# First transfers, token copies and bias stores of an attention and expert kernel, put in another order

## The chip, the cores and the metric

The kernel runs on one core of a Trainium2 chip. The core has a matrix engine (TensorE, "PE" in the profile, with its weight loads as "PEld"), a vector engine (VectorE, "DVE"), ScalarE ("ACT"), GpSimd ("POOL") and SyncE ("SP"), which here only issues DMA. ScalarE and GpSimd issue DMA as well. Each engine runs its own queue of instructions in order; semaphores tie the queues together. The metric is the device time of one execution in microseconds, and the median over the executions is what counts.

## The reference

The computation has two parts: an attention over 16 sequences of 512 tokens (width 512, 16 heads of 64, one shared key and value head, a null key, an additive bias and a causal mask), and a layer of 16 experts in which each expert picks its own 512 tokens. The tokens `x` themselves are added to the result.

```python
xn = layernorm(x, g_in)
q = (xn @ Wq).reshape(b, n, H, DH).transpose(0, 2, 1, 3) * scale
kv = xn @ Wkv                              # k, v: one head, with a null key and value put in front
sim = einsum('bhid,bjd->bhij', q, k) + bias
sim = where(causal_mask, neg, sim)         # causal, the same for all sequences
sim = where(mask_p[:, None, None, :], sim, neg)
out = einsum('bhij,bjd->bhid', softmax(sim), v) @ Wo
a = layernorm(out, g_out)
...
logits = rmsnorm(a) @ router_weight.T + router_bias
_, idx = top_k(logits.T, 512)              # each of 16 experts takes 512 of the 8192 tokens
y = gelu(xe @ fc1.T + b1) @ fc2.T + b2     # per expert
output = scatter_add(y * gates) / gate_sums
return x + output
```

The bias (16 heads, 512 x 512) is the same for every sequence; so is the causal mask, and so is their combination.

## The kernel before, in words

**Attention: 16 sequences of 8 head pairs.** A loop over `p` = 0 to 128 handles pair `p` (sequence `p // 8`, two heads) and, in the same turn, parts of its neighbours. For pair `p` TensorE makes the scores in PSUM (`sp`), VectorE adds the bias and takes the row minimum in one instruction (`reduce`, four query blocks in the order 3, 2, 0, then 1), ScalarE takes the exponentials and normalizes. In the next turn (`behind`) VectorE transposes the probabilities in squares of 32 x 32 (`turn`: six instructions into the buffer `sq`, of which there is only one), and 16 DMAs of 80 KB move the squares to their places (`move`, `sq` to `pt`): ten are issued by SP and six by POOL. In the turn after that (`turned`) TensorE multiplies them with the values (`attend`, `ap`). Beside this the turn makes the queries of the next pair (`qp`), normalizes and transposes the token tiles of the next sequences (`InNorm`, with its inverse root `ln_r` on POOL), and projects and routes the previous sequence.

**Order.** The helper class `Pinned` (line 119) keeps what TensorE, VectorE, ScalarE and GpSimd are given in the order of the program text. SP is not pinned: `nc.sync` is ordered by the scheduler of the framework. A tile that has a fixed number of buffers makes its next writer wait for the last reader: two for a token tile `x`, two for a bias tile.

**Bias.** `load_bias(p)` (line 227) is called in turn `p - 1`. For the first eight pairs it loads 1280 KB (1.3 MB) of bias, has POOL fill the upper triangle of the four diagonal blocks with a large negative number (`affine_select`), and stores the result to the memory tensor `causal`; from pair 8 on the masked bias is loaded from there. In POOL's order these four masks of pair `p + 1` stand ahead of the six moves of turn `p`; the store is issued by SP.

**Tokens.** `Sequence.load` (line 251) loads a tile of 128 tokens (256 KB) into SBUF and copies it from there to the output, so that the experts can later add to it. The first sequence's four tiles are loaded ahead of the loop, the next one's also before the loop, the others two turns ahead of their normalization.

**Constants.** ScalarE issues all the weight loads at the start (lines 163 to 184): input gain, key and value weights, null key and value, 2 MB of query weights, the null bias, 2 MB of output weights `wo`, the gains and the router. VectorE then negates `vk_col` and the null bias (`nn_sb`), makes the first sequence's mask (`km`), and only then starts the first normalizations (lines 610 to 618). The transposed tokens (`turn`, line 259) pass through one PSUM buffer.

**Experts.** After attention and the choice of tokens come 16 experts, in which the two layers' products follow one another on TensorE; nothing in that part is touched.

Of the kernel before, what the change touches and what calls it, by code (L numbers as in the profile page):

```python
# [8 lines left out]
F32 = mybir.dt.float32  # L9
# [4 lines left out]
AF = mybir.ActivationFunctionType  # L14
ALU = mybir.AluOpType
# [4 lines left out]
P = 128  # L20
EPS = 1e-5

BIG = float(2.0**100)
# [3 lines left out]
def tile_adaln_ffn(  # L27
# [36 lines left out]
    scale = DH ** -0.5  # L64
# [21 lines left out]
    causal = dram.tile([HP, P, 2, SW], F32, name="causal")  # L86
# [22 lines left out]
        base=-1, channel_multiplier=-1,  # L109
# [9 lines left out]
    class Pinned:  # L119
# [4 lines left out]

        def __getattr__(self, name):
            made = getattr(self.engine, name)
            return lambda *args, **kwargs: tc.keep_in_program_order(made(*args, **kwargs))  # L127

    te, ve, se, ge = [Pinned(a) for a in (nc.tensor, nc.vector, nc.scalar, nc.gpsimd)]


    with ExitStack() as st:
# [27 lines left out]
        rw_sb = const.tile([P, DC, E], F32, name="rw_sb")  # L160
        rb_sb = const.tile([P, E], F32, name="rb_sb")

        nc.scalar.dma_start(out=g_in_sb, in_=g_in)
        for j in range(2):
            nc.scalar.dma_start(
                out=wvk_sb[:, :, j * DH : (j + 1) * DH], in_=wkv_c[:, :, (1 - j) * DH : (2 - j) * DH]
            )
            nc.scalar.dma_start(
                out=vk_col[j * DH : (j + 1) * DH, :],
                in_=null_kv[1 - j].rearrange("(d o) -> d o", o=1),  # L170
            )
        for c in range(DC):
            nc.scalar.dma_start(out=wq_sb[:, c, :], in_=wq[c * P : (c + 1) * P, :])
        nc.scalar.dma_start(out=nb_sb, in_=null_bias.partition_broadcast(P))

        for j in range(2):
            nc.scalar.dma_start(
                out=nv_col[j * DH : (j + 1) * DH, :], in_=null_kv[1].rearrange("(d o) -> d o", o=1)
            )
        nc.scalar.dma_start(out=wo_sb, in_=wo.rearrange("(c p) n -> p c n", p=P))  # L180
        nc.scalar.dma_start(out=g_out_sb, in_=g_out.partition_broadcast(P))
        nc.scalar.dma_start(out=nw_sb, in_=norm_w.partition_broadcast(P))
        nc.scalar.dma_start(out=rw_sb, in_=router_w.rearrange("(c p) e -> p c e", p=P))
        nc.scalar.dma_start(out=rb_sb, in_=router_b.partition_broadcast(P))

        mhalf = const.tile([P, 1], F32, name="mhalf")
        nc.vector.memset(mhalf, -0.5)
# [38 lines left out]

        def load_bias(p):


            bt = biasp.tile([P, 2, SW], F32, name=f"bias_{p}", tag="bias")  # L230
            if p >= HP:
                nc.sync.dma_start(out=bt, in_=causal[p % HP])
                return bt
            nc.sync.dma_start(out=bt, in_=bias[p])
            for q in range(QB):
                diag = bt[:, :, off[q] + ext[q] - P : off[q] + ext[q]]
                ge.affine_select(
                    out=diag, in_=diag, pattern=[[0, 2], [-1, P]],
                    compare_op=ALU.is_ge, fill=-BIG, base=0, channel_multiplier=1,
                )  # L240
            nc.sync.dma_start(out=causal[p], in_=bt)
            return bt

        class Sequence:

# [5 lines left out]
            def load(self, t):  # L251
                b = self.b
                rows = slice(b * N + t * P, b * N + (t + 1) * P)
                xt = work.tile([P, D], F32, name=f"x_{b}_{t}", tag="x")
                nc.sync.dma_start(out=xt, in_=x_t[rows, :])
                nc.sync.dma_start(out=out_t[rows, :], in_=xt)
                self.xts[t] = xt

            def turn(self, t):
                if t == 0:  # L260
                    self.xnt = seq.tile([P, DC, N], F32, name=f"xnt_{self.b}", tag="xnt")
                tp = ps_t.tile([P, DC, P], F32, name=f"xtp_{self.b}_{t}", tag="t")
                for c in range(DC):
                    te.transpose(tp[:, c, :], self.xns[t][:, c * P : (c + 1) * P], ident)
                ve.tensor_tensor(
                    self.xnt[:, :, t * P : (t + 1) * P], tp,
                    g_in_sb.unsqueeze(2).to_broadcast([P, DC, P]), ALU.mult,
                )

            def mask(self):  # L270
                m8 = small.tile([DH + 1, N], U8, name=f"m8_{self.b}", tag="m8", bufs=1)
# [335 lines left out]
        for t in range(QB):  # L607
            seqs[0].load(t)
        biases = {0: load_bias(0)}
        ve.tensor_scalar_mul(vk_col, vk_col, -1.0)  # L610
        ve.tensor_scalar_mul(nn_sb, nb_sb, -1.0)
        seqs[0].mask()
# [17 lines left out]
        for p in range(B * HP + 1):  # L630
            b, hp = divmod(p, HP)
            now, ahead = ahead, None
            if p + 1 < B * HP:
                biases[p + 1] = load_bias(p + 1)
                ahead = Pair(seqs[(p + 1) // HP], (p + 1) % HP)
            for c, t in loads.get(p, ()):
                seqs[c].load(t)
            bt = biases.pop(p, None)
            chains = [InNorm(seqs[c], t) for c, t in ins.get(p, ())]
            if p in norms:  # L640
                chains.append(OutNorm(seqs[norms[p][0]], norms[p][1]))
            second = steps(*[seqs[c].project(*divmod(h, 2)) for c, h in halves.get(p, ())])
            asked = ahead.queries() if ahead else steps()

            if now:
                now.scores(3)
                now.scores(2, 0)
                now.reduce(3, bt)
                now.exps(3)
# [53 lines left out]
        ve, se, ge = nc.vector, nc.scalar, nc.gpsimd  # L703
        for t in range(QB):
            last.project_part(t, range(early, HP))
            n = OutNorm(last, t)
# [609 lines left out]
```

## Time and profile before

| | |
|---|---|
| median of 3 runs | 3651.52 us (3649.92 to 3652.57) |
| profiled execution | 3655.35 us, its span 3653.6 us |
| mean granted TensorE clock | 0.977 |
| PE busy | 3441.1 us (94%) |
| DVE busy | 2330.9 us (64%) |
| ACT busy | 1585.2 us (43%) |
| POOL busy | 894.3 us (24%) |
| first score matmul of pair 0 | 49.5 us |
| first score matmul of pair 8 | 171.1 us |
| end of attention | about 1940 us |
| SP's DMA queue | 473.44 MB, 39.0% of 16 engines' span |
| POOL's DMA queue | 101.29 MB, 12.3% |
| ACT's DMA queue | 5.53 MB, 0.4% |

Busy times overlap, since the engines work beside each other. What an engine's idle time costs depends on who waits for it, so the profile is read by stages: TensorE has gaps in the first 200 us and between about 1940 and 2130 us, and is full elsewhere. Queues named SPq, ACTq and POOLq show the issue of a DMA, not its movement of data.

### The profile page before, as it was taken

The page shows a single profiled execution, that of the slowest core. Times are in us where ns is not written, and L with a number is a line of the kernel's source. Part 1 is how long each engine was busy: PE and PEld are TensorE (multiplying, and loading weights), DVE is VectorE, ACT ScalarE, POOL GpSimd, SP SyncE. Part 2 cuts the span into 40 slices and gives each one's busy share as a digit, 9 for nine tenths or more (in the row PEclk, how much of TensorE's full clock was granted, in tenths as well). Part 3 has the DMA queues.
Part 4 walks back from the last instruction along what each step waited for, and adds up shares of the span by engine and source line. Part 5 has one row for each costly group of instructions (what it writes and reads, how often), then busy time and mean ns, then how long its engine had stood idle before and what let it go on. Part 6 is the DMA issues. An engine that isn't in the chain of part 4 may idle for free.

```text
span 3653.6 us, 52226 instructions
## 1 busy us (share of the span) xinstructions
PE 3441.1 (94%) x16972; PEld 2478.7 (68%) x16972; DVE 2330.9 (64%) x6028; ACT 1585.2 (43%) x4152; POOL 894.3 (24%) x1314
## 2 busy tenths in 40 slices
PE   5799999999999999999993699999999999999998
PEld 2355556555565555555552488888888888888887
DVE  4567676777667767767656865555565666555553
ACT  3567676676666766667660111111121111111111
POOL 2232332332332323233320222111121122222110
PEclk9799999999999999999996799999999999999999
DMA  7777666676667676676642233333333334333330
GB/s 251 241 212 225 207 205 209 211 221 214 203 208 222 213 212 205 205 214 198 196 148 104 70 118 110 104 93 94 115 122 119 119 122 122 110 122 110 112 91 12
DMA packets 263286, 583.58 MB, mean 160 GB/s; under 512 B 49255, under 2 KB 118023, under 8 KB 245607
## 3 DMA queue, kind: packets, MB, share of 16 engines
q1 hardware_dynamic: 215680, 473.44, 39.0%
q0 software_dynamic: 42960, 101.29, 12.3%
q10 hardware_dynamic: 4375, 5.53, 0.4%
q8 instruction: 136, 2.23, 0.3%
q14 instruction: 135, 1.11, 0.1%
HBM read 349.64 MB, written 61.87 MB: 113 GB/s over the span
## 4 chain that ended last, share of the span: by engine, by line
PE 50%; DVE 5%; issue 1%; DMA 1%; POOL 0%; ACT 0%; SPq 0%; DVEq 0%; POOLq 0%; ACTq 0%
PE r_y L127 9%; PE pc L127 6%; PE pc_y L127 6%; PE pa_y L127 6%; PE pa L127 6%; PE pe L127 3%; PE pb L127 3%; PE pd L127 3%; PE op L127 2%; PE qp L127 2%; PE sp L127 1%; PE ap L127 1%; DVE sel L836 1%; PE xgp L127 1%; DVE sq L127 1%
## 5 line engine op out<-in xcount | busy, mean ns | idle before, releaser
L127 ACT ACTIVATE p<-p,nm 128x512 f32<-128x512 f32 (+3 forms) x1024 | 561.9, 550 | 243.8 <-DVE nm L127 242.5
L127 DVE CUSTOM_DVE_ANT_0 p<-sp,bias,nn_sb 128x512 f32<-128x512 f32 (+3 forms) x1024 | 500.5, 546 | 174.1 <-PE sp L127 174.0
L127 POOL DMA_DIRECT2D pt<-sq x762 | 381.6, 508 | 877.6 <-issue 559.8
L127 PE MATMUL qp<-xnt,wq_sb 128*128 128x512 f32 x1024 | 512.2, 623 | 0.0
L127 PE MATMUL op<-wo_sb,ot 128*128 128x256 f32 x1920 | 457.0, 382 | 8.8 <-ACT ot L127 8.6
L127 PEld LDWEIGHTS op<-wo_sb,ot 128*128 128x128 f32 x1920 | 357.4, 190 | 109.3 <-issue 54.3
L127 DVE STREAM_TRANSPOSE sq<-p 128x896 f32<-128x896 f32 x762 | 398.7, 589 | 49.8 <-DMA pt<-sq 27.5
L127 ACT ACTIVATE p<-p,rs 128x512 f32<-128x512 f32 (+2 forms) x768 | 406.2, 603 | 1.9 <-DVE rs L127 1.1
L127 POOL DMA_INDIRECT out_dram<-y,tok x64 | 106.2, 1659 | 1184.3 <-ACT y L1145 1184.3
L1053 ACT ACTIVATE h<-h,b_sb 128x512 f32<-128x512 f32 (+1 forms) x256 | 143.4, 607 | 529.1 <-DVE h L127 471.1
L127 PE MATMUL sp<-ka,qa 64*128 64x512 f32 (+3 forms) x2048 | 357.7, 440 | 1.8 <-ACT qa L127 1.8
L127 PE MATMUL ap<-pt,vp 128*64 128x512 f32 (+3 forms) x2048 | 310.8, 446 | 18.6 <-DMA pt<-sq 9.1
L1145 ACT ACTIVATE y<-y,gg 128x512 f32<-128x512 f32 x64 | 46.2, 722 | 647.3 <-DVE y L127 647.3
L127 PEld LDWEIGHTS qp<-xnt,wq_sb 128*128 128x128 f32 x1024 | 174.9, 190 | 183.2 <-issue 167.8
L127 PEld LDWEIGHTS ap<-pt,vp 128*64 128x64 f32 x2048 | 148.8, 139 | 195.4 <-issue 158.1
L127 PE MATMUL pa<-xe,w 128*128 128x256 f32 x1024 | 243.5, 381 | 0.0
L127 PEld LDWEIGHTS sp<-ka,qa 64*128 64x128 f32 x2048 | 174.2, 190 | 87.5 <-issue 81.5
L127 PE MATMUL pa_y<-w,h 128*128 128x256 f32 x1024 | 231.5, 379 | 0.0
L127 PE MATMUL r_y<-w2t,hs 128*128 128x256 f32 x1024 | 231.5, 379 | 0.0
L127 PEld LDWEIGHTS pa<-xe,w 128*128 128x128 f32 x1024 | 195.9, 191 | 27.0
L127 PEld LDWEIGHTS r_y<-w2t,hs 128*128 128x128 f32 x1024 | 194.6, 190 | 26.5
L127 PEld LDWEIGHTS pa_y<-w,h 128*128 128x128 f32 x1024 | 193.4, 190 | 25.7
(191 smaller groups left out, 5191.6 us busy)
## 6 DMA issues: line engine op xcount, KB each, us to landing
bias<-causal SPq DMA_DIRECT2D x120, 1280.0 KB
w<-in_fc_dram SPq DMA_DIRECT2D x256, 512.0 KB
pt<-sq SPq DMA_DIRECT2D x1270, 80.0 KB
pt<-sq POOLq DMA_DIRECT2D x762, 80.0 KB
x<-in_x_dram SPq DMA_DIRECT2D x64, 256.0 KB
out_dram<-x SPq DMA_DIRECT2D x64, 256.0 KB
table<-xf SPq DMA_DIRECT2D x64, 256.0 KB
bias<-in_bias_dram SPq DMA_DIRECT2D x8, 1280.0 KB
```

The source lines that it names most:

```text
L127: return lambda *args, **kwargs: tc.keep_in_program_order(made(*args, **kwargs))
L836: nc.vector.tensor_scalar(flags, l2, than, None, op, ALU.add, accum_out=red)
L1053: nc.scalar.activation(a[0], a[1], AF.Gelu, bias=b1_sb[:, self.e, f : f + 1])
L1145: nc.scalar.activation(y, y, AF.Copy, scale=self.gg[:, g, self.e : self.e + 1])
```

## The change

- The four token tiles of the first sequence become SP's first transfers, into four buffers of their own (`x` and `xf`). ScalarE now issues only the key and value weights, the input gain and the query weights, these in two parts by columns (the first two pairs' first). The small vectors are issued by POOL. `wo`, the gains and the router weights go to `later_weights`, issued by POOL in turn 1.
- The first normalizations stand ahead of `nn_sb`, `km` and `vk_col` on VectorE. The first sequence's odd tiles go through another PSUM pool and are scaled by ScalarE in four pieces.
- SP is pinned too (`sy`), so its transfers keep the order of the text.
- `load_bias` only loads. `mask_bias(p + 1)` stands behind the moves of turn `p`; POOL masks and then issues the store to `causal`.
- Token tiles are no longer copied to the output from SBUF. In turns 8 to 71 SP copies one tile of 128 rows from the input tensor to the output tensor, memory to memory, behind its moves. Token loads stand behind the moves too, and the second half of the second sequence is loaded in turn 0 instead of before the loop.

TensorE's instructions keep their order.

```diff
+            def call(*args, **kwargs):
+                self.last = tc.keep_in_program_order(made(*args, **kwargs))
+                return self.last
...
+    te, ve, se, ge, sy = [
+        Pinned(a) for a in (nc.tensor, nc.vector, nc.scalar, nc.gpsimd, nc.sync)
+    ]
...
-        nc.scalar.dma_start(out=g_in_sb, in_=g_in)
+        x0 = {}
+        for t in range(QB):
+            x0[t] = work.tile([P, D], F32, name=f"x_0_{t}", tag="x" if t < 2 else "xf")
+            nc.sync.dma_start(out=x0[t], in_=x_t[t * P : (t + 1) * P, :])
...
-        for c in range(DC):
-            nc.scalar.dma_start(out=wq_sb[:, c, :], in_=wq[c * P : (c + 1) * P, :])
-        nc.scalar.dma_start(out=nb_sb, in_=null_bias.partition_broadcast(P))
+        for cols in (slice(0, 2 * P), slice(2 * P, H * DH)):
+            nc.scalar.dma_start(out=wq_sb[:, :, cols], in_=wq_c[:, :, cols])
...
+        nc.gpsimd.dma_start(out=nb_sb, in_=null_bias.partition_broadcast(P))
...
+        def later_weights():
+            ge.dma_start(out=wo_sb, in_=wo.rearrange("(c p) n -> p c n", p=P))
+            ge.dma_start(out=g_out_sb, in_=g_out.partition_broadcast(P))
+            ge.dma_start(out=nw_sb, in_=norm_w.partition_broadcast(P))
+            ge.dma_start(out=rw_sb, in_=router_w.rearrange("(c p) e -> p c e", p=P))
+            ge.dma_start(out=rb_sb, in_=router_b.partition_broadcast(P))
...
-            nc.sync.dma_start(out=causal[p], in_=bt)
+            sy.dma_start(out=bt, in_=causal[p % HP] if p >= HP else bias[p])
             return bt
+        def mask_bias(p, bt):
+            with tc.issue_after(ge.last.ins):
+                for q in range(QB):
+                    diag = bt[:, :, off[q] + ext[q] - P : off[q] + ext[q]]
+                    ge.affine_select(
...
+            ge.dma_start(out=causal[p], in_=bt)
...
-                nc.sync.dma_start(out=xt, in_=x_t[rows, :])
-                nc.sync.dma_start(out=out_t[rows, :], in_=xt)
+                sy.dma_start(out=xt, in_=x_t[rows, :])
...
+                if odd:
+                    for c in range(DC):
+                        se.activation(dst[:, c, :], tp[:, c, :], AF.Copy, scale=g_in_sb[:, c : c + 1])
...
-            loads.setdefault(max(p - 2, -1), []).extend(tiles)
+            loads.setdefault(max(p - 2, min(p - 1, 0)), []).extend(tiles)
...
         for pair in ((0, 1), (2, 3)):
...
+        mask_bias(0, biases[0])
+        ve.tensor_scalar_mul(vk_col, vk_col, -1.0)
         for t in range(QB):
             seqs[0].turn(t)
+        ve.tensor_scalar_mul(nn_sb, nb_sb, -1.0)
+        seqs[0].mask()
...
-                behind.move(nc.sync, range(6, SN * SN))
+                behind.move(sy, range(6, SN * SN))
                 behind.move(ge, range(6))
+            if p + 1 < HP:
+                mask_bias(p + 1, biases[p + 1])
+            if p == 1:
+                later_weights()
+            if 0 <= p - HP < NT // P:
+                rows = slice((p - HP) * P, (p - HP + 1) * P)
+                sy.dma_start(out=out_t[rows, :], in_=x_t[rows, :])
+            for c, t in loads.get(p, ()):
+                seqs[c].load(t)
```

More of the change, by code (lines that the diff above doesn't have):

```diff
@@ L126, in __getattr__ @@
             made = getattr(self.engine, name)
-            return lambda *args, **kwargs: tc.keep_in_program_order(made(*args, **kwargs))
-    te, ve, se, ge = [Pinned(a) for a in (nc.tensor, nc.vector, nc.scalar, nc.gpsimd)]
+            def call(*args, **kwargs):
+                self.last = tc.keep_in_program_order(made(*args, **kwargs))
+                return self.last
+            return call
+    te, ve, se, ge, sy = [
+        Pinned(a) for a in (nc.tensor, nc.vector, nc.scalar, nc.gpsimd, nc.sync)
+    ]
     with ExitStack() as st:
@@ L167, in tile_adaln_ffn @@
             )
-            nc.scalar.dma_start(
+        nc.scalar.dma_start(out=g_in_sb, in_=g_in)
+        wq_c = wq.rearrange("(c p) n -> p c n", p=P)
+        for cols in (slice(0, 2 * P), slice(2 * P, H * DH)):
+            nc.scalar.dma_start(out=wq_sb[:, :, cols], in_=wq_c[:, :, cols])
+        for j in range(2):
+            nc.gpsimd.dma_start(
                 out=vk_col[j * DH : (j + 1) * DH, :],
@@ L171, in tile_adaln_ffn @@
             )
-        for c in range(DC):
-            nc.scalar.dma_start(out=wq_sb[:, c, :], in_=wq[c * P : (c + 1) * P, :])
-        nc.scalar.dma_start(out=nb_sb, in_=null_bias.partition_broadcast(P))
+        nc.gpsimd.dma_start(out=nb_sb, in_=null_bias.partition_broadcast(P))
         for j in range(2):
-            nc.scalar.dma_start(
+            nc.gpsimd.dma_start(
                 out=nv_col[j * DH : (j + 1) * DH, :], in_=null_kv[1].rearrange("(d o) -> d o", o=1)
             )
[L180 to L184, printed above, removed]
+        def later_weights():
[4 more added lines that the diff above has]
+            ge.dma_start(out=rb_sb, in_=router_b.partition_broadcast(P))
         mhalf = const.tile([P, 1], F32, name="mhalf")
@@ L230, in load_bias @@
             bt = biasp.tile([P, 2, SW], F32, name=f"bias_{p}", tag="bias")
[L231 to L241, printed above, removed]
-            return bt
+            sy.dma_start(out=bt, in_=causal[p % HP] if p >= HP else bias[p])
+            return bt
+        def mask_bias(p, bt):
[3 more added lines that the diff above has]
+                    ge.affine_select(
+                        out=diag, in_=diag, pattern=[[0, 2], [-1, P]],
+                        compare_op=ALU.is_ge, fill=-BIG, base=0, channel_multiplier=1,
+                    )
+            ge.dma_start(out=causal[p], in_=bt)
         class Sequence:
@@ L261, in turn @@
                     self.xnt = seq.tile([P, DC, N], F32, name=f"xnt_{self.b}", tag="xnt")
-                tp = ps_t.tile([P, DC, P], F32, name=f"xtp_{self.b}_{t}", tag="t")
+                odd = self.b == 0 and t % 2 == 1
+                pool, tag = (ps_m, "m") if odd else (ps_t, "t")
+                tp = pool.tile([P, DC, P], F32, name=f"xtp_{self.b}_{t}", tag=tag)
                 for c in range(DC):
                     te.transpose(tp[:, c, :], self.xns[t][:, c * P : (c + 1) * P], ident)
[L265 to L268, printed above, removed]
+                dst = self.xnt[:, :, t * P : (t + 1) * P]
+                if odd:
+                    for c in range(DC):
+                        se.activation(dst[:, c, :], tp[:, c, :], AF.Copy, scale=g_in_sb[:, c : c + 1])
+                else:
+                    ve.tensor_tensor(
+                        dst, tp, g_in_sb.unsqueeze(2).to_broadcast([P, DC, P]), ALU.mult
+                    )
             def mask(self):
@@ L604, in tile_adaln_ffn @@
         for p, tiles in ins.items():
-            loads.setdefault(max(p - 2, -1), []).extend(tiles)
-        for t in range(QB):
-            seqs[0].load(t)
+            loads.setdefault(max(p - 2, min(p - 1, 0)), []).extend(tiles)
+        seqs[0].xts = x0
         biases = {0: load_bias(0)}
-        ve.tensor_scalar_mul(vk_col, vk_col, -1.0)
-        ve.tensor_scalar_mul(nn_sb, nb_sb, -1.0)
-        seqs[0].mask()
         for pair in ((0, 1), (2, 3)):
@@ L635, in tile_adaln_ffn @@
                 ahead = Pair(seqs[(p + 1) // HP], (p + 1) % HP)
-            for c, t in loads.get(p, ()):
-                seqs[c].load(t)
             bt = biases.pop(p, None)
@@ L702, in tile_adaln_ffn @@
         last = seqs[end]
-        ve, se, ge = nc.vector, nc.scalar, nc.gpsimd
+        ve, se, ge, sy = nc.vector, nc.scalar, nc.gpsimd, nc.sync
         for t in range(QB):
```

## The prediction

> **What bounds the kernel now.** I read the windows of busy time first, to find where TensorE is not full; then, in those places, the instructions in order of time, engine by engine.
>
> ```profile
> 50.00:100.00 50.00, 37.61 (x167) 16.64 (x168) 34.54 (x116) 30.80 (x93) 11.62 (x25) 0.88 0.70 228
> 100.00:150.00 50.00, 35.44 (x152) 16.97 (x151) 26.06 (x84) 26.95 (x72) 14.24 (x32) 0.84 0.73 232
> 150.00:200.00 50.00, 41.67 (x192) 20.62 (x194) 32.23 (x106) 29.81 (x84) 14.67 (x31) 0.87 0.77 240
> ...
> 500.00:1000.00 500.00, 491.73 (x2590) 291.04 (x2590) 353.07 (x1164) 350.33 (x975) 158.69 (x280) 1.00 0.69 212
> ```
>
> The columns are stretch, its length, busy time of PE, weight loads, DVE, ACT and POOL, granted clock, DMA share, GB/s. From 200 us to the end of attention (about 1940 us) PE is 98% busy: nothing in its instruction order changes, so there I count zero. Up to 200 us it is not full and its clock falls below 1.0. A loss there is never made up, so a gain there comes out at the end one for one. Two things leave it empty. The first is the start:
>
> ```profile
> 19.48 0.17 DVE L127 TENSOR_SCALAR nn_sb<-nb_sb 128x16 f32<-128x16 f32 x1 [8.29 <-DMA nb_sb<-in_null_bias_dram]
> 20.42 0.69 DVE L127 BATCH_NORM_STATS2 ln_s<-x 128x6 f32<-128x512 f32 x1
> 23.23 1.76 SPq L255 DMA_DIRECT2D x<-in_x_dram  x2
> 29.41 0.69 DVE L127 BATCH_NORM_STATS2 ln_s<-x 128x6 f32<-128x512 f32 x1 [4.77 <-DMA x<-in_x_dram]
> 38.60 5.93 PE L127 MATMUL kp<-xnt,wvk_sb 128*128 128x256 f32 x16
> ```
>
> Each row: start, duration, instruction, and in brackets the idle time before it with what ended it. The first normalization (20.42) stands in DVE's queue behind the negated null bias, whose transfer lies behind 2 MB of wq. Token tiles 2 and 3 are asked for only at 23.23, when two buffers come free. The second is pairs 2 to 7:
>
> ```profile
> 76.47 3.14 DVE L127 STREAM_TRANSPOSE sq<-p 128x896 f32<-128x896 f32 x6 [0.76 <-DMA pt<-sq]
> 79.64 0.51 SPq L517 DMA_DIRECT2D pt<-sq  x1
> 82.33 0.34 SPq L256 DMA_DIRECT2D out_dram<-x  x1
> 82.99 0.39 SPq L241 DMA_DIRECT2D causal<-bias  x1
> 83.42 9.36 SPq L517 DMA_DIRECT2D pt<-sq  x9
> 92.90 0.52 SPq L234 DMA_DIRECT2D bias<-in_bias_dram  x1
> 95.24 3.14 DVE L127 STREAM_TRANSPOSE sq<-p 128x896 f32<-128x896 f32 x6 [9.20 <-DMA pt<-sq]
> 95.27 4.54 PE L127 MATMUL ap<-pt,vp 128*64 128x512 f32 x16 [7.27 <-DMA pt<-sq]
> ```
>
> This is one turn of a loop: transposed squares, ten moves on SP (six on POOL beside them), landing, next transposes, since there is one squares buffer. After the first move SP waits for a token tile, then for the mask, issues the 1.3 MB store, and its other nine moves queue behind that store at 1.04 us each.
>
> **The loop in numbers.** Call T_k the start of pair k's transposes: T_0 to T_6 are 63.28, 76.47, 95.24, 112.44, 131.57, 150.84, 166.93. From T_1 to T_6 a pair takes 90.5/5 = 18.1 us. From the end of the transposes (T_k + 3.1) to the end of the last SP move: 13.2, 12.0, 13.9, 13.7 and 11.3 us for k = 1 to 5. But 8.4 for k = 0 (66.45 to 74.80: the store had gone ahead at 64.33 and nothing stood among the moves), and 7.0 in a later pair without stores:
>
> ```profile
> 625.45 3.13 DVE L127 STREAM_TRANSPOSE sq<-p 128x896 f32<-128x896 f32 x6
> ...
> 628.65 6.89 SPq L517 DMA_DIRECT2D pt<-sq  x10
> ```
>
> From the last move to the next transposes it takes 2.5, 2.1, 2.1, 2.4, 1.6, mean 2.1.
>
> **The change, part by part.**
>
> *Start.* The four token loads go first on SP, 0.43 each: all issued by 2.5 us. DMA moved 203 GB/s in 0 to 5 us and 304 in 5 to 10, so 1.0 and 2.5 MB by then; if ScalarE's queue (wvk, wq) takes half, the 1.05 MB of tokens are through when 2.1 MB are, at 8.6, and landed at about 10.5 (estimate; ends 8.6 and 12). The second pair of normalizations took 29.41 to 33.24 = 3.8, so xn_3 is ready at 14.4; the last turn is 1.11, and the key matmuls start at 15.5 instead of 38.60. The two turns given to ScalarE (eight pieces; the nearest row, its copy of 128x256, 0.37) end under the first half of those matmuls, 2.9 us. The five small loads that POOL now issues (0.5 each by its moves) end before the first ln_t, so they cost nothing; without that cover, 2.5. From there to the first score reduction, 12.8 us (38.60 to 51.41), nothing moves. **Gain 23** (ends 20 and 25).
>
> *Bias 1 and 2.* Bias 1 is now issued behind the ka moves, near 23; with two token tiles ahead it is 1.8 MB, at 383 GB/s (65 to 70 us) 4.8, landed about 30, masked by 32; pair 1 wants it at 60.32 - 23 = 37.3. Cost 0, cover 5. Bias 2 stands on SP behind two token loads that wait for the pair 0 normalization (60.0 - 23 = 37.0): issued 38.4, landed about 45. Its mask waits for POOL's moves of pair 0 (to 47) and ends at 48.5; pair 2 wants it at 49.7. Cost 0, cover 1.
>
> *The later weights at pair 1, a new wait.* POOL now has, behind that mask: the store, five weight loads, and only then two ln_r. Each load costs between 0.5 (a move, 32 rows) and 2.82 (the POOL store of the gate table, 64-byte pieces); I take 0.8, since wo has many pieces but far fewer than that table. So 48.5 + 0.5 + 4 + 1.2 = 54.2, where before (71.18 - 23) it was 48.2. DVE's xn is in order and everything behind it, pair 2's reductions and transposes, is late by 6.0 less the 0.8 that T_1 waited anyhow: **cost 5.3** (ends 3.7 and 15). Nothing hides it.
>
> *The loop.* The store leaves SP for POOL, behind the moves and the mask; the copy of tokens to the output leaves the first eight pairs. What remains on SP in pair k is bias, ten moves, a token load. So the moves take between 7.0 (no store about) and 12.8 (as now, if it is DMA load); I take 8.4, the row of k = 0, where a store was in flight. A turn is then 3.1 + 8.4 + 2.1 = 13.6 us, five turns 68.0: **gain 22.5** (ends 0 and 29.5). What is late next? The mask: bias issued at E, the end of the moves, lands at about E + 6; POOL's moves end at E + 8.2, mask E + 9.7, reductions 3.1, so transposes from E + 12.8, against E + 2.1 + 13.6 = E + 15.7 for the loop. DMA is next: moves alone ran at 202 GB/s on 0.82 of the engines (70 to 75 us), so 1.31 MB are 5.3 us; bias and store at some 410 GB/s 3.2 each; with tokens 12 us of 13.6. wo and its neighbours, 2.6 MB or 6.5 us, fall into this: **cost 2** (0 to 6.5), the rest in the idle share.
>
> *Memory to memory.* 64 copies of 256 KB were on SP before and are after, one per pair from pair 8 to 71. The issue is 0.37 either way; waits of 37 us on SP for token tiles (300 to 1000 us) go, which PE did not feel. The copy itself has no row: 0.65 us at 400 GB/s, double if reading and writing memory add up. The loop there is 3.1 + 7.0 + 2.1 = 12.2 in a pair of 14.0 (611.41 to 625.45), a slack of 1.8, so cost 0. The bounds: at best PE's named waits from 300 to 1900 us, 27; at worst the rival below.
>
> Sum: 23 - 5.3 + 22.5 - 2 = **38 us**. Against the profiled execution's 3655.4 that is 3617; the median shown is 3651.5, 3.8 below that execution, and the change takes the same piece off it: **3614**.
>
> **Two rules against the rows.** The Trainium skill, "DMA: Bandwidth & Descriptors", section "Issuing engines are not separate DMA queues", says that transfers from several engines share the same DMA engines, and spreading them only saves issue time. By it the eight moved stores save 8 x 0.35 = 2.8 us of SP's time and the loop stays at 18.1: 3636. The rows say that SP's order, not only its bytes, makes 8.4 into 13. "SBUF — State Buffer", section "SBUF: two separate sides" (its "DVE blocks DMA" trap, with the figures just below it), says that GpSimd cannot write descriptors while VectorE, in some modes, holds the port pair they share, 620 ns becoming about 3100. By it the five weight loads cost 2.5 more each: 12.5 more, 3626. Here 762 POOL moves lasted 496 / 496 / 763 ns (least, median, most), beside a DVE busy 71% of the time: I take the row.
>
> **The rivals.**
> - *The loop stays DMA-bound.* For it: the share reached 0.91 in 65 to 81 us, and all 1.3 MB stores stay. Against: 0.73 on the whole, and k = 0. Then 23 - 5.3 - 2 = 16: 3636.
> - *Moves run as in later pairs and the weights issue at 0.5.* 23 - 3.7 + 29.5 = 49: 3603. Against: the store is there.
> - *Slower: the memory-to-memory copies sit in SP's ring ahead of the next bias and moves.* If one costs c, each of 64 pairs loses c - 1.8. It eats the 38 us from c = 2.4; at c = 3 the loss is 77: 3690. For it: no row shows such a copy. Against: 256 KB at the 202 GB/s of the moves would be 1.3.
> - *Little comes of it:* weights, stores and tokens collide and return the start's gain: 3650.
>
> **How the numbers follow.** Forecast 0.60 (3604 to 3625), DMA-bound loop 0.18, faster moves 0.12, little 0.05, slower 0.05. The range 3600 to 3636 takes in the forecast, half of the third and most of the second. A measurement can tell 0.2%, 7 us, from no change: faster 0.93, same 0.03, slower 0.04.
>
> **What would show it.** Key matmuls at 15 to 18 us; POOL's ln_r of pair 1 behind five loads, with a DVE wait of some 6 us; transposes from T_1 to T_6 13 to 14.5 apart; no store among SP's moves; PE clock nearer 1.0 in 100 to 200 us; the later stretch at 98%. It is wrong if transposes stay 17 or more apart, or if pairs 8 to 71 grow longer than those from 72 on.

## The result, and the profile after

The kernel after takes **3618.99 us** (median of 5 runs, 3616.58 to 3623.88) against 3651.52 (3649.92 to 3653.55): ratio 0.9913, 95% interval 0.9899 to 0.9927, a gain of 32.5 us. Its profiled execution took 3619.08, its span 3617.4; between the two spans lie 36.2 us, 3.8 of which are the amount by which the profiled execution of before lies above its median.

The windows of busy time after (columns as before):

```profile
0.00:50.00 50.00, 31.72 (x134) 17.10 (x135) 28.52 (x124) 22.07 (x61) 21.67 (x47) 0.99 0.80 270
50.00:100.00 50.00, 36.09 (x164) 16.50 (x164) 30.89 (x97) 27.60 (x76) 16.38 (x36) 0.84 0.97 303
100.00:150.00 50.00, 41.73 (x178) 18.47 (x179) 33.92 (x115) 31.99 (x90) 14.80 (x31) 0.86 0.79 259
150.00:200.00 50.00, 49.00 (x254) 27.15 (x251) 36.96 (x121) 37.20 (x105) 15.54 (x29) 1.00 0.78 239
```

The first stretch of before was

```profile
0.00:50.00 50.00, 14.74 (x46) 9.45 (x46) 13.70 (x66) 2.99 (x5) 7.22 (x21) 1.00 0.73 271
```

So TensorE is twice as busy in the first 50 us and full from 150 on, 50 us earlier. But in 50 to 100 it is no busier than before, and the DMA share rose to 0.97: that is the place to look at. The start first, from the timeline:

```profile
3.79 0.69 DVE L129 BATCH_NORM_STATS2 ln_s<-x 128x6 f32<-128x512 f32 x1 [0.86 <-DMA x<-in_x_dram]
13.44 2.73 PE L129 MATMUL kp<-xnt,wvk_sb 128*128 128x256 f32 x9
```

The first tokens land before 3.8, all four normalizations are through by 11, and the key matmuls start at 13.44 instead of 38.60. Then pair 1:

```profile
43.91 1.49 POOL L129 TENSOR_SCALAR_AFFINE_SELECT bias<-bias 128x256 f32<-128x256 f32 x4 [0.79 <-DMA bias<-in_bias_dram]
45.70 0.58 POOL L129 DMA_DIRECT2D causal<-bias  x1 [0.30 <-POOL bias L129]
46.28 0.92 POOL L129 DMA_DIRECT2D wo_sb<-in_wo_dram  x1
...
49.55 1.21 POOL L129 TENSOR_TENSOR ln_r<-ln_t,mhalf 128x1 f32<-128x1 f32 x2
50.18 1.16 DVE L129 TENSOR_SCALAR xn<-x,ln_mv,ln_r 128x512 f32<-128x512 f32 x2 [6.82 <-POOL ln_r L129]
56.49 3.14 DVE L129 STREAM_TRANSPOSE sq<-p 128x896 f32<-128x896 f32 x6 [1.20 <-DMA pt<-sq]
59.66 7.23 SPq L129 DMA_DIRECT2D pt<-sq  x10
...
62.80 0.50 POOL L129 DMA_DIRECT2D pt<-sq  x1 [1.33 <-DMA wo_sb<-in_wo_dram]
```

Mask, store and five loads stand ahead of ln_r on POOL, and VectorE waits 6.82 us for it, idle while the loads are issued. SP's ten moves take 7.23 us with nothing among them, where before nine of them took 9.36 behind the store. POOL's fourth move waits for wo to land. Over all of 37 to 140 us, VectorE's wait for ln_r is

```profile
DVE xn L129 <- POOL ln_r L129: 21.2, 4, 6.8
```

(what waited and for what, us in total, times, longest).

To see where the 36.2 us come from, I compare T_k, the starts of the large transposes, with those of before. "Lead" is before less after.

| | T_0 | T_1 | T_6 | T_11 | T_71 | T_126 | span |
|---|---|---|---|---|---|---|---|
| lead, us | 26.6 | 20.0 | 32.8 | 34.1 | 29.3 | 28.3 | 36.2 |

So the start gave 26.6, pair 1 took 6.6 back, the loop from T_1 to T_6 gave 12.8 (77.7 us instead of 90.5), pairs 6 to 11 another 1.3, and pairs 11 to 71 took 4.8. The last 7.9 us are gained behind attention, in code that the change does not touch: 3.7 up to the start of the last scatter, 4.2 behind it. They belong to the one execution of before that was traced: its experts took 1591.6 us and its end behind the last scatter's start 10.2, where all thirteen other traces have 1585.6 to 1586.7 and 5.6 to 6.1. As that execution lies only 3.8 us above its median, leads against it come out too small by about the rest: 28.3 at T_126, where the medians give 32.5.

### The profile page after: what moved, and what is told of

Read it like the earlier page. It is cut to its first block, busy times and chain, and to the rows that moved or that the text cites. A ratio compares the mean times of both kernels' runs of the same rounds, so it can differ in the third digit from the quotient of the medians.

```text
span 3617.4 us, 52129 instructions
## 1 busy us (share of the span) xinstructions
PE 3436.0 (95%) x16972; PEld 2477.8 (68%) x16972; DVE 2326.7 (64%) x6026; ACT 1588.6 (44%) x4160; POOL 904.7 (25%) x1332
## 4 chain that ended last, share of the span: by engine, by line
PE 79%; DVE 8%; DMA 3%; SPq 3%; issue 2%; ACT 1%; POOL 1%; DVEq 0%; POOLq 0%; ACTq 0%
PE op L129 10%; PE r_y L129 9%; PE qp L129 9%; PE sp L129 7%; PE pa L129 6%; PE pc L129 6%; PE pc_y L129 6%; PE pa_y L129 6%; PE ap L129 6%; PE pd L129 3%; PE pe L129 3%; PE pb L129 3%; SPq L129 3%; DVE sq L129 2%; PE xfp L129 2%; DVE p L129 2%
## 5 line engine op out<-in xcount | busy, mean ns | idle before, releaser
L129 PEld LDWEIGHTS pa<-xe,w 128*128 128x128 f32 x1024 | 195.6, 191 | 26.8
```

The lines of the kernel that those rows point to most:

```text
L129: self.last = tc.keep_in_program_order(made(*args, **kwargs))
```

## The experiments

All twelve were measured in three groups, each beside the kernel before on the same chip (medians there 3649.86, 3650.10 and 3650.75). Ratios are to that.

| run | what | us | ratio (95%) | lead T_0, T_1, T_6, T_11, T_71, T_126 |
|---|---|---|---|---|
| e1 | after, token copies left out | 3612.42 | 0.9899 (0.9882, 0.9915) | 25.0, 17.9, 30.2, 32.8, 35.9, 33.9 |
| e2 | after, norms ahead on POOL | 3617.58 | 0.9916 (0.9900, 0.9933) | 25.3, 25.1, 31.2, 31.7, 29.8, 29.4 |
| e3 | before + loop part | 3645.83 | 0.9989 (0.9980, 0.9998) | -0.5, -2.1, 7.6, 5.9, 3.9, 2.5 |
| e4 | before, store on POOL | 3643.66 | 0.9985 (0.9978, 0.9992) | -0.6, -1.6, 5.4, 4.2, 3.3, 3.2 |
| e5 | after, weights at pair 3 | 3623.52 | 0.9924 (0.9908, 0.9941) | 26.0, 23.6, 27.7, 28.2, 26.3, 23.9 |
| e6 | e2, weights at pair 7 | 3616.27 | 0.9902 (0.9886, 0.9919) | 25.9, 22.8, 40.4, 34.3, 27.5, 26.8 |
| e7 | e6, copies unordered | 3616.08 | 0.9908 (0.9891, 0.9924) | 25.4, 24.4, 40.5, 31.7, 34.4, 33.3 |
| e8 | before + start part | 3656.86 | 1.0016 (1.0009, 1.0023) | 10.3, 2.0, -1.8, -1.4, -9.4, -12.5 |
| e9 | e6, weights by ScalarE | 3619.11 | 0.9912 (0.9897, 0.9928) | 25.8, 26.1, 42.1, 34.7, 30.0, 30.6 |
| e10 | e9, copies in the routing | 3639.35 | 0.9970 (0.9959, 0.9982) | 26.1, 25.9, 43.3, 35.7, 36.2, 37.5 |
| e11 | e8 + first mask moved | 3648.06 | 0.9991 (0.9983, 1.0000) | 22.3, 14.3, 9.4, 8.9, -0.4, -3.4 |
| e12 | e3 + token copies moved | 3633.34 | 0.9953 (0.9938, 0.9968) | -1.4, -3.3, 8.6, 10.8, 10.6, 12.6 |

Leads are those of one traced execution each to the one of before; but for e10, the gain by the medians is 0.7 to 7 us more than the lead at T_126.

**e1: what do the copies cost?**

```diff
-            if 0 <= p - HP < NT // P:
-                rows = slice((p - HP) * P, (p - HP + 1) * P)
-                sy.dma_start(out=out_t[rows, :], in_=x_t[rows, :])
```

> The changed kernel without its 64 memory-to-memory copies (the tokens are not copied to the output, so the result lacks them). In the changed kernel the lead over the kernel before falls from 34.1 us at pair 11 to 29.3 at pair 71 and is 31.3 at pair 90. If the copies cost this (some 0.08 us per pair, through a fuller DMA), the lead stays near 34 and the time is about 3614, 5 below the changed kernel. If the fall has another cause (token loads behind the moves, chance of one execution), the time stays at 3619 within 2.

The lead, which fell by 4.8 us from T_11 to T_71 in the kernel after, grew by 3.1. The waits of VectorE from 240 to 1120 us say how. After:

```profile
DVE km L129 <- DMA m<-in_mask_dram: 13.0, 4, 4.1
DVE p L129 <- DMA bias<-causal: 7.4, 6, 2.2
```

Both lines are absent without copies, where the largest DMA wait of VectorE is

```profile
DVE sq L129 <- DMA table<-xf: 2.4, 3, 1.0
```

A copy stands in SP's order ahead of the next bias (and mask row), and these land late. TensorE's wait before the next sequence's keys (`kp`) goes with the late bias over the same stretch: 11.6 us in the kernel after, 7.0 in e1. In after, e2, e5, e6 and e9 it is 7.9 to 12.5, with waits for the bias of 4.9 to 9.0; in e1, e7, e10 and e12, which have no such wait, 6.9 to 7.1. That is the mechanism of the slower rival, at a far smaller price: 0.1 us per pair. That the copies cost this is shown by e1; the way over the bias rests on these waits going together. On the medians the difference is 5 us by the ratios, whose intervals overlap; the leads are what carries it.

**e2: is ln_r, behind mask and store, what makes a turn 15.5 us?** `mask_bias` and `later_weights` move behind the chains' first half:

```diff
             for n in chains:
                 n.a()
+            if p + 1 < HP:
+                mask_bias(p + 1, biases[p + 1])
+            if p == 1:
+                later_weights()
```

> The changed kernel with GpSimd's mask, store and later weights issued behind the inverse roots of the turn instead of ahead of them. If VectorE's waits for ln_r (6.8 us in pair 1, 6.5, 4.0 and 4.0 in pairs 4 to 6) are what keeps the loop at 15.5 us instead of the 13.6 of the forecast, they shrink below 1 us each, T_1 comes 5 to 6 earlier and T_1 to T_6 takes about 70 instead of 77.7: some 12 us in all, 3607. If the loop is bound by DMA load, the waits only move to the squares or to the mask: 3615 to 3619.

T_1 came 5 us earlier, and from T_2 to T_6 a turn took 14.2 us, where the kernel after took 15.9. But T_1 to T_2 took 27.6. POOL and VectorE there:

```profile
54.81 1.01 POOL L129 DMA_DIRECT2D pt<-sq  x2 [2.23 <-DVE sq L129]
58.87 0.50 POOL L129 DMA_DIRECT2D pt<-sq  x1 [3.05 <-DMA causal<-bias]
69.30 0.50 POOL L129 DMA_DIRECT2D pt<-sq  x1 [9.93 <-DMA wo_sb<-in_wo_dram]
...
73.08 1.48 POOL L129 TENSOR_SCALAR_AFFINE_SELECT bias<-bias 128x256 f32<-128x256 f32 x4
74.60 0.75 DVE L129 CUSTOM_DVE_ANT_0 p<-sp,bias,nn_sb 128x512 f32<-128x512 f32 x1 [16.29 <-POOL bias L129]
```

The third move waits for the store, the fourth for wo, each the transfer that POOL issued eight before it. The trace shows why: POOL's 1037 transfers signal their landing by eight semaphores in turn, and each first waits for the one that used its semaphore before. SP and ScalarE have another eight together. So the limit lies in how these programs are built; whether an engine has one of its own, no run shows. The next mask stands behind, and VectorE waits 16.29 us for that. ln_r had held the turns; ahead of it, the weights' landing takes its place.

**e3 and e4: the loop part by itself, and of it only the engine that stores.** e4 is one line in the kernel before; e3 also moves the mask behind the moves.

```diff
-            nc.sync.dma_start(out=causal[p], in_=bt)
+            ge.dma_start(out=causal[p], in_=bt)
```

> The kernel before with the loop's part of the change alone: mask behind the moves, store issued by GpSimd; start, token copies and weights as before. If this part gives what the forecast put on it, T_1 to T_6 takes 68 to 78 us instead of 90.5 and the time is 3629 to 3639 (gain 13 to 22). If the pace in the changed kernel comes from the token copies that left the first eight pairs, it stays near 90 and the time is 3645 to 3651.

> The kernel before with one line changed: the masked bias is stored by GpSimd instead of SyncE; the mask stays ahead of GpSimd's six moves. If the store among SP's moves made them slow, the ten moves take 8 to 9 us instead of 12 to 14 and the gain is nearly that of moving the mask as well (10 to 18 us, 3633 to 3641). If the mask ahead of GpSimd's moves made the loop long, the six moves still wait for the bias and the gain is under 5. If the rule holds that another issuing engine saves only issue time, the gain is under 3.

e4 gained 6 us and e3 4, within each other's intervals. T_1 to T_6 took 83.5 and 80.8 us against 90.5, which is 7.0 and 9.7 of the 12.8; at T_1 both were behind by some 2. One turn of e4 shows what was left among the moves:

```profile
78.08 3.15 DVE L127 STREAM_TRANSPOSE sq<-p 128x896 f32<-128x896 f32 x6 [2.02 <-DMA pt<-sq]
81.26 0.52 SPq L517 DMA_DIRECT2D pt<-sq  x1
83.11 0.34 SPq L256 DMA_DIRECT2D out_dram<-x  x1
83.50 9.00 SPq L517 DMA_DIRECT2D pt<-sq  x9
84.16 0.61 POOL L127 DMA_DIRECT2D causal<-bias  x1 [0.30 <-POOL bias L127]
```

The store is gone from SP. The copy of a token tile to the output still holds nine moves until the tile has landed, and these still take 1.00 us each, now beside a store of POOL. From the end of the transposes to the end of SP's last move, a turn of pairs 1 to 5 took on average:

| us | before | e4 | e3 | e12 | after |
|---|---|---|---|---|---|
| the ten moves themselves | 8.8 | 9.2 | 7.7 | 6.9 | 7.0 |
| stops ahead of and between them | 4.1 | 1.3 | 1.4 | 1.3 | 0.8 |

So the store's place on SP cost the stops and not the pace of the moves. In the stops SP waited for the mask ahead of the store (before, 60 to 170 us: 4.9 us in five) and for token tiles ahead of their copies (9.0 in four). The scheduler orders SP in e4 as in before, and without the store these copies and loads, too, stood among the moves of two pairs instead of three. The pace rose when mask and store went behind the moves (e3), and more when the token copies left (e12).

**e12: the loop part with the token copies moved.** e3, and in it the copy from SBUF taken out and the 64 copies memory to memory put in.

```diff
-                nc.sync.dma_start(out=out_t[rows, :], in_=xt)
...
+            if 0 <= p - HP < NT // P:
+                rows = slice((p - HP) * P, (p - HP + 1) * P)
+                nc.sync.dma_start(out=out_t[rows, :], in_=x_t[rows, :])
```

> The kernel before with the loop part of the change (mask behind the moves, store on POOL) and with the token copies taken out of the first eight pairs and made from memory to memory from pair 8 on; start as before. The loop part alone gained 6 us at T_11 and 4 at the end. Theory (the other half of the loop's 12.8 us came from the copies that left SP's queue): T_1 to T_6 at 77 to 79 us (90.5 before, 80.7 with the loop part alone), lead of 11 to 13 at T_11, of which the copies take back 6 by pair 71: 3643 to 3646 at the end. Rival (the copies out of SP's queue give nothing in these pairs): lead of 6 or less at T_11, and 3648 to 3654.

T_1 to T_6 took 78.6 and the lead at T_11 is 10.8, about as the theory had it. But it holds to T_71, and the gain is 17.4 us, some 10 more than expected. In the kernel after the copies took the lead down, here not: they have their late mask rows here too (km waited 19.4 us in 5 from 240 to 1120), but no wait of VectorE for the bias. So late mask rows alone cost nothing. Why the bias comes in time here is not settled.

**e8 and e11: the start by itself.** e8 is the start part on the kernel before: tokens first, queues as in the change, weights at pair 1 on POOL, odd turns through ScalarE. The first token copies stay on SP behind the first loads, the mask of bias 0 stays in `load_bias`. The core of it, and then what e11 changes: the first bias's mask goes behind the normalizations.

```diff
+            x0[t] = work.tile([P, D], F32, name=f"x_0_{t}", tag="x" if t < 2 else "xf")
+            nc.sync.dma_start(out=x0[t], in_=x_t[t * P : (t + 1) * P, :])
+        for t in range(QB):
+            nc.sync.dma_start(out=out_t[t * P : (t + 1) * P, :], in_=x0[t])
...
+            if p == 1:
+                later_weights()
```

```diff
+        with tc.issue_after(ge.last.ins):
+            mask_bias(0, biases[0])
         ve.tensor_scalar_mul(vk_col, vk_col, -1.0)
```

> The kernel before, with the start part of the change alone: tokens first on SP into buffers of their own, wvk and wq next on ScalarE's queue, small vectors on POOL, later weights at pair 1 on POOL, two turns through ScalarE, negations behind the normalizations. Mask ahead, store and token copies on SP as before. Theory of the prediction's terms: T_0 25 to 27 us earlier, the loop's turns as before (18 us from T_1 to T_6), less 3 to 6 us for the weights ahead of ln_r: 3627 to 3633. Rival (the start only shifts the jam: with less time since the launch, biases, weights and tokens of pairs 1 to 7 are late and the turns grow): lead at T_6 below 15 us, 3636 to 3648.

> The start part alone on the kernel before, once more, now with the first bias's mask behind the normalizations of the first tokens, as the change has it; in the run without this, POOL held the first ln_r behind that mask until bias 0 landed (13.6 us of wait, bias landed at 19.3), and the key matmuls began at 28.5 instead of 13.4. Masks and stores of pairs 1 to 7 and the token copies stay as before. Theory A (the terms add: 26 us at the start, less 3 to 6 for the weights): key matmuls at 13 to 15, T_0 at 37, lead at T_6 20 us or more, 3627 to 3633. Theory B (the loop of pairs 0 to 7 is held by SP's queue and the transfers in it, and a start that comes earlier only waits longer there; only with the loop part does it reach the end): T_0 at 37, lead at T_6 below 12, 3640 to 3655.

e8 came out slower than before, which neither theory had. Its POOL at the start:

```profile
19.32 1.47 POOL L129 TENSOR_SCALAR_AFFINE_SELECT bias<-bias 128x256 f32<-128x256 f32 x4 [13.63 <-DMA bias<-in_bias_dram]
20.76 1.19 POOL L129 TENSOR_TENSOR ln_r<-ln_t,mhalf 128x1 f32<-128x1 f32 x2
```

The first two token tiles were there by 4.9, and ln_r stood behind a mask that waits for bias 0. So the position of that one mask is 15 us of the start: the key matmuls began at 28.54 in e8 and at 13.49 in e11. In e11 T_0 came 22.3 us early, and theory B held: 8.0 of it were gone at T_1, 12.9 at T_6. The waits of VectorE over pairs 0 to 6, before and then in e11:

```profile
DVE sq L127 <- DMA pt<-sq: 12.1, 3, 9.2
```

```profile
DVE sq L129 <- DMA pt<-sq: 30.1, 5, 10.7
```

(50 to 170 us of before, 37 to 160 of e11.) In e11 the transposes wait for moves on SP that stand behind stores and token copies: the ten moves end 16.2, 17.8, 18.8 and 15.0 us after T_2 to T_5, against 15.1, 17.1, 16.8 and 14.5 before, and 9.5 to 12.7 after. Both e8 and e11 lose another 11 to 12 us between T_11 and T_126, though from pair 2 on every engine's order is that of before; TensorE waits longer for the outputs `ot` (from 232 us on 11.8 instead of 6.9 us for `op` in e8). The cause of that part is open.

**e5, e6, e9: where do the later weights cost nothing?** e5 has them at pair 3 in the kernel after (`p == 3`), e6 at pair 7 in e2 (first lines below), e9 is e6 with ScalarE issuing all five (last lines).

```diff
-            if p == 1:
+            if p == 7:
                 later_weights()
...
-            ge.dma_start(out=wo_sb, in_=wo.rearrange("(c p) n -> p c n", p=P))
+            se.dma_start(out=wo_sb, in_=wo.rearrange("(c p) n -> p c n", p=P))
```

> The kernel after, with its five later weight loads issued by POOL behind pair 3's mask and store instead of pair 1's (pairs 2 and 3 have no token chain behind them). Theory (the loads cost time because two ln_r stand behind their 4 us of issue, and because POOL's next moves wait for them to land): the DVE wait for ln_r in pair 1 falls from 6.8 us to about 3 (mask and store still ahead), T_0 to T_1 falls from 19.8 us to about 16, the moves of pair 2 issue without waiting for wo; the blocked moves appear in pair 4 instead, behind no ln_r. Net gain over after 3 to 6 us: about 3613 to 3616. Rival (the place does not matter, DMA is short of 6.5 us for those 2.6 MB wherever they stand): T_1 comes earlier and the same amount is lost by T_6, time 3617 to 3621.

> The kernel before this one in the study that put mask, store and loads behind the chains' first half (so ln_r goes ahead on POOL), now with the later weights at pair 7, where POOL has no mask and no store any more. That earlier one gained 5 us at T_1 and lost it again from T_1 to T_2 (27.6 us), since POOL's moves waited for the landing of wo and its neighbours, and mask 3 waited behind them. Theory (those two are one and the same jam, and moving the loads frees it): T_1 at about 51, T_1 to T_6 at 70 to 73 us (14.2 a turn), hence T_6 near 122 to 125 instead of 134.2; of these 9 to 12 us some come back in pairs 8 to 10 where the weights now land, so 3607 to 3612. Rival (the turns of 15 us are DMA's): T_6 not before 130 and 3614 to 3619.

> The kernel with the norms ahead on POOL and the later weights at pair 7, with these five loads issued by ScalarE instead of POOL. In every kernel so far that issued them on POOL, the pair behind them stood still: its fourth to sixth move waited on POOL for wo, g_out and nw to land (T_1 to T_2 27.6 us with the weights at pair 1 and norms first, T_3 to T_4 23.5 with the weights at pair 3, T_6 to T_7 19.5 with the weights at pair 7, other turns 13 to 16). Theory (POOL's outstanding transfers block it, not DMA's bytes): T_6 to T_7 falls to 13 to 15 us, no POOL wait for wo, ScalarE loses about 2.5 us of issue once; 5 to 6 us below the version with POOL, 3609 to 3612. Rival (DMA is short of the 6.5 us that 2.6 MB take): T_7 no earlier than 144, 3614 to 3618.

They cost something everywhere. In e5, T_0 to T_1 fell to 15.6 as expected, which puts the weights' part of that turn in the kernel after at 4.2 us; T_3 to T_4 took 23.4, 6.0 more than there. There VectorE waited 12.45 us for an ln_r behind POOL's blocked moves:

```profile
95.53 0.50 POOL L129 DMA_DIRECT2D pt<-sq  x1 [6.28 <-DMA wo_sb<-in_wo_dram]
...
102.17 0.55 DVE L129 TENSOR_SCALAR xn<-x,ln_mv,ln_r 128x512 f32<-128x512 f32 x1 [12.45 <-POOL ln_r L129]
```

In e6 the lead had grown to 40.4 us at T_6, and T_6 to T_7 took 19.5, 7.2 more than in the kernel after. Here no queue was blocked, and the rival held:

```profile
129.70 8.25 SPq L129 DMA_DIRECT2D pt<-sq  x10
133.67 1.11 POOL L129 DMA_DIRECT2D wo_sb<-in_wo_dram  x1
145.99 3.14 DVE L129 STREAM_TRANSPOSE sq<-p 128x896 f32<-128x896 f32 x6 [8.17 <-DMA x<-in_x_dram]
...
140.00:145.00 5.00, 0.00 (x0) 0.00 (x0) 0.00 (x0) 0.00 (x0) 0.00 (x0) 0.71 1.03 315
```

All ten moves were issued by 137.96, but the last landed at 145.3 (the bracket names a token load that shares a semaphore with a move). For 5 us every engine stood still at a DMA share of 1: the moves share the DMA engines with 2.6 MB of weights and, from 138.74 on, the next bias.

e9 does not decide it. POOL is not blocked there, yet T_6 to T_7 took 21.6, for two other queues were:

```profile
SPq L129 <- DMA wo_sb<-in_wo_dram: 9.2, 1, 9.2
...
141.13 0.21 ACT L129 ACTIVATE ne<-ne 128x8 f32<-128x8 f32 x1 [11.65 <-DMA pt<-sq]
141.37 0.17 DVE L129 TENSOR_TENSOR sm<-sm,ne 128x8 f32<-128x8 f32 x1 [11.53 <-ACT ne L129]
...
135.00:140.00 5.00, 0.00 (x0) 0.00 (x0) 0.00 (x0) 0.00 (x0) 0.00 (x0) 0.54 1.05 279
```

(The first line is what SP waited for from 110 to 150 us.) The five loads took their semaphores from those that ScalarE shares with SP. So four of them waited for moves to land, with ScalarE's part of the sums `ne` behind them and VectorE behind that; and SP's ninth move waited until wo had landed.

**e7 and e10: the copies elsewhere.** Both issue them as 16 copies of 1 MB by SP, in the text behind the first expert's weights; e10 also holds them there in SP's order.

```diff
     first = weights(0)
+    with tc.issue_after(last_load[0].ins):
+        for i in range(16):
+            rows = slice(i * NT // 16, (i + 1) * NT // 16)
+            last_copy = nc.sync.dma_start(out=out_t[rows, :], in_=x_t[rows, :])
```

> The same as the last one (norms ahead on POOL, weights at pair 7), and the 64 copies of tokens to the output taken out of pairs 8 to 71 and issued as 16 copies of 1 MB by SP behind the first expert's weights, in the stretch of about 1950 to 2045 us where TensorE and DMA are nearly idle (DMA share 0.05 from 1950 to 2000). Theory (in the loop the copies cost about 6 us, there they are hidden): 6 us below the run without this step, 3601 to 3606. Rival (they delay something there, the table of counts that the routing writes and reads at about 2045, or the next expert's weights): no gain, or a loss of up to 30 us, seen as a later first expert.

> The same (norms first, weights at pair 7 on ScalarE), and the token copies held behind the first expert's weights on SP, as 16 copies of 1 MB, by an explicit order this time: in the earlier try they had no order, and left between 7 and 361 us, in the very pairs where DMA is full. Theory (copies cost about 6 us beside attention and are hidden in the routing stretch, where the DMA share is 0.05): 6 us below the run without this step, 3602 to 3607, the lead grows or holds from pair 8 to 71, and the first expert starts no later relative to the end of attention. Rival (the routing's writes and reads of its table at 2030 to 2060 queue behind 17 MB of copies): the first expert starts 10 to 40 us later, 3615 to 3650.

e7 did not do what it was meant to: nothing orders the copies, and they left between 7 and 361 us. After that the lead grew (31.7 at T_11, 34.4 at T_71), as without copies. e10 kept its lead through attention (35.7, 36.2, 37.5), where e9, the same kernel with copies in pairs 8 to 71, fell from 34.7 to 30.0: once more some 5 us for the copies. Then it lost 27:

```profile
1934.96 65.37 SPq L790 DMA_DIRECT2D out_dram<-in_x_dram  x16
...
2024.12 1.09 POOL L129 DMA_INDIRECT cg<-ctab,ridx  x1 [111.55 <-DMA ctab<-upto]
```

SP's part of the table write lies behind the copies, the first gather starts at 2024 instead of 2003, and the first expert 20.3 us later than in e9, though attention ended 7 earlier. But the copies did not fill those 65 us. SP's waits from 1930 to 2005 us:

```profile
SPq L790 <- DMA ctab<-upto: 47.9, 1, 47.9
```

Eight copies were issued by 1947.5. The ninth had the semaphore of ScalarE's part of the table write, which came at 1992.1, so SP stood still until 1995.4, and the other eight left just ahead of its own part of the table, at 2001.1. Whether the copies would be free in that stretch, where the DMA share was 0.20 from 1960 to 1990, is therefore not tested.

No variant of the kernel after is faster than it by more than the intervals.

## Why the prediction was right

The total was forecast at 3614 and came at 3619. Some of that closeness is luck: the loop gave 9.7 us less than forecast and the token copies cost 5, against a start that gave 3.6 more and smaller gains beside it. By its steps:

- **Start, 23.** 26.6 at T_0. The tokens landed earlier than estimated; the rest of the chain was as counted.
- **"A gain there comes out at the end one for one."** This failed as a general statement. The same start on the loop of before (e11) leads by 22.3 at T_0, by 9.4 at T_6, and is worth 2.7 us at the end. The start's gain survives only with the rest of the change, which takes away what it would queue behind. The loop part and the copies alone are worth 17.4 (e12), the start alone 2.7 (0 to 6.2 by its interval), the whole change 32.5. So the terms are not a sum; but the kernel after also pins SP and puts the token loads behind the moves, which neither e11 nor e12 has (in e12 a load still stands among the moves of pair 3, which take 11.0 us, 7.7 in the kernel after). How much of the 12 us by which the whole exceeds the two belongs to that is not measured.
- **The later weights at pair 1, 5.3, and wo's data, 2.** 6.6 from T_0 to T_1, with an ln_r wait of 6.82 where 6.0 was worked out. Well sized together, though 2.4 of the 6.6 are the mask and store ahead of ln_r, which stay when the weights go (e5). That the weights cost 6 us and more in other places too, e5 and e6 showed.
- **The loop, 22.5.** This is the mis-sized term: 12.8. "The moves take ... I take 8.4" held: 6.2 to 9.5 us in pairs 1 to 6. "Landing, 2.1" did not: from the last move to the next transposes it took 3.5 to 6.5 us from T_1 to T_6, since in pairs with token chains ln_r stands behind mask and store on POOL: from 37 to 140 us VectorE waited for it four times, 21.2 us in all, 6.8 of them in pair 1. With ln_r ahead, turns were 14.2 us (e2), near the forecast of 13.6, and 1.8 below the kernel after over the same four turns: 7.1 of the 9.7 us. The prediction had counted this order for pair 1 only, and had asked what is late next of the mask and of DMA, not of ln_r. Its reading that nine moves "queue behind that store at 1.04 us each" was half right: with the store on POOL (e4) they took 1.00 each, and what went were the stops.
- **Token copies, 0.** Measured 5 us, by e1 against the kernel after and by e10 against e9: the next bias lands late. The slower rival named the place, but its c - 1.8 per pair counted only moves.
- **The first mask.** The prediction passed over it; e8 shows that without its move the key matmuls start at 28.5, 15 us of the 23.
- **The rules.** By the Trainium skill's "DMA: Bandwidth & Descriptors", section "Issuing engines are not separate DMA queues", the moved stores would save 2.8 us and the turn stay at 18.1. e4, that move alone, gave 6.2 us (2.9 to 8.0 by its interval, so the rule's figure is just outside) and turns of 16.7; with the mask behind the moves and the token copies out as well (e12) they are 15.7. The moves themselves went no faster in e4, which agrees with the page; what its figure leaves out is SP's stops, 2.8 us of a turn. The stretching of POOL's loads to some 3.1 us by the Trainium skill's "SBUF — State Buffer", section "SBUF: two separate sides", is not seen: the five took 0.56 to 0.92 us each in the kernel after, where VectorE was idle, and as long in e2, where it was busy all that time with reductions and transposes. Whether these are of the modes that the page means, no run shows.

Of the signs named ahead, the key matmuls came earlier than said, ln_r stood behind the loads with a wait near 6, and no store was among the moves; TensorE's clock is 1.00 in 150 to 200 us but still 0.86 in 100 to 150. Transposes 13 to 14.5 apart did not come (15.5), and pairs 8 to 71 did grow longer, by 0.08 us a pair (14.37 to 14.45), where those from 72 to 119 stayed at 14.37 to 14.38: one of the two signs of being wrong came true, for some 5 us in all.

## What to carry to other kernels

An earlier start is worth only what the stage behind it can take in: measure the two together and each alone before adding their gains. When a queue is freed of one obstacle, list everything that stands ahead of each small, needed instruction on every engine (here ln_r, 0.6 us of work behind a mask that waits for a transfer), in all turns and not in the first alone. Bulk transfers without a deadline still delay the deadlines of others in the same queue, so place them by order, not by where they stand in the text. And look at the semaphores: a transfer can be held by one that has nothing to do with it but uses the same semaphore, on another engine too (e9, e10).

## What the runs showed of the hardware

- In these programs a transfer of POOL waited for the one issued eight before it, whose semaphore it takes over: in the kernel after, in e2 and in e5 a move waited so for causal, wo, g_out or nw, up to 9.93 us. SP and ScalarE share eight in the same way: up to 9.2 us in e9, 47.9 in e10.
- A copy of 256 KB from memory to memory landed a median of 3.6 us after its issue in e12 and 3.4 in e9, and 64 of them cost the loop about 5 us.
- With 2.6 MB of weights beside the moves, a DMA share of about 1 meant 277 to 279 GB/s (e9) or 315 (e6), where in the stretch of before from 65 to 70 us it was 383: how long DMA is full does not follow from the bytes alone.
